# A conditioned two-part block on one core: conditioning bias from compact rows, a seeded fourth output tile, and a re-ordered weight load

## The chip, the cores and the metric

The kernel runs on one core of one Trainium2 chip. The core has five engines with instruction queues of their own: TensorE (PE: matrix products; PEld is its weight load), VectorE (DVE), ScalarE (ACT), GpSimd (POOL) and SyncE (SP, which here only issues transfers). Each runs its instructions in order and waits on counters that the others raise. Sixteen DMA engines move data between memory (DRAM) and on-chip memory; products land in PSUM banks. The metric is the device time of one execution in microseconds.

## The reference

```python
m = mask[:, :, None]                                   # x: 32 x 128 x 512, mask: 32 x 128
emb = silu(t) @ ada_w + ada_b                          # t: 32 x 512, ada_w: 512 x 1536
shift, scale, gate_msa = split(emb, 3, axis=1)
norm = layernorm(x) * (1 + scale[:, None]) + shift[:, None]
norm = where(m, norm, 0)
fwd = gelu(norm @ ssm_w1 + ssm_b1) @ ssm_w2 + ssm_b2
bwd = ...                                              # the same with the bwd_ weights
x = x + gate_msa[:, None] * where(m, fwd + bwd, 0)
ff_ada = silu(t) @ ffada_w + ffada_b
shift_mlp, scale_mlp, gate_mlp = split(ff_ada, 3, axis=1)
ff_norm = layernorm(x) * (1 + scale_mlp[:, None]) + shift_mlp[:, None]
h = gelu_tanh(ff_norm @ ff_w1 + ff_b1)                 # 512 x 1024
return x + gate_mlp[:, None] * (h @ ff_w2 + ff_b2)     # 1024 x 512
```

All is float32. The first part changes only the tokens whose mask is set, at most the last 32 of a sequence of 128. The second part is done for all 4096 tokens.

## The kernel before

**First part.** The masked tokens are gathered into 512 slots, four tiles of 128 (an indirect transfer by POOL, L281). Tiles 0 and 1 (group s0) go first, tiles 2 and 3 (s1) follow. Each group is normalised, transposed (`transposed_slots`, L192), sent through the hidden layer (`ph_s`, L656 and L207) and through the output product `project` (L217: eight matmuls of 128x512 into a bank `po_s`, half of them on `ssm_w2`, half on `bwd_w2`). A bank can be *seeded*: ACT copies the bias `b2` into it beforehand (L236), and the product adds onto it. In the kernel before, tiles 0 to 2 are seeded; tile 3 is not, its bank comes from another pool, and `finish_late` (L1364) adds `b2` on DVE. The finished rows go to DRAM: `x1_wide` (tiles 0 and 1, L368, read back at L792 for the first eight sequences) and `x1_rows` (all four, L369 and L1371, read back by POOL's eight gathers of `take_first_half`, L864).

**Conditioning.** `modulation_matmuls` (L299) makes shift, scale and gate for all 32 batches: for each of four column blocks j, 32 output partitions, sixteen matmuls of 32 columns for the four row blocks k of `ada_w`. `modulation_rows` (L311) adds the bias on DVE, from a tile in which each bias row stands on 32 partitions (`load_conditioning_bias`, L129: one broadcast transfer of 64 KB for each of three rows, twice). `pm_ss` is shift and scale of the first part, `pm_g` its gate, `pm_f` all three of the second part, `mod1` and `mod2` the results. `keep_clock` (L596) issues matmuls whose result nobody reads.

**Second part.** Both products are done by blocks: seven products P1 to P7 in place of eight, at two levels in the first product. There, seven *streams* (order 1, 2, 5, 6, 3, 7, 4) of seven products each run over the tokens of a pair of sides; there are four pairs. Streams 5, 6, 7 and 4 use sums of weight blocks, which DVE makes (L715), SP stores to `t_rows` (L719, L720) and `load_weights` (L1037, its transfer is L1042, tile `tw`) reads back. `token_sums` (L1015, `sx` and `xn_sy`) makes the token side on DVE. After P5 of a stream, `with_p5` (L1144) adds two 128x512 blocks on POOL at L1147; `after` (L1171) adds another on POOL at L1176. The result of a POOL sum goes through DVE (L1121 after P6; `seed`, L1136, at L1140 before P2) into the bank that the next product adds onto.

**What sets the order.** From L428 on the order of every engine is the order of the program text (a schedule by hand). Each transfer on the queues of SP and ACT takes one of eight completion counters in turn, and a transfer waits until the one that had its counter before has landed.

Around the switch from the first part to the second, SP issues in this order: load of `fw2` (L136), six stores of weight sums (L719, L720), two stores of `x1_rows` (L369), `b2_row`, `fb2`, two loads of x (L396), two stores of `x1_rows` (L1371), `tw` for stream 5 (L1042), two loads of x, `tw` for stream 6.

Of the kernel before, what the change touches and what calls it, by code (L numbers as in the profile page):

```python
# [9 lines left out]
F32 = mybir.dt.float32  # L10
# [4 lines left out]
ALU = mybir.AluOpType  # L15
# [7 lines left out]
def kernel(  # L23
# [49 lines left out]
    nc = tc.nc  # L73
    B, S, D = x.shape
    P = 128
# [3 lines left out]
    KC = D // P  # L79
# [46 lines left out]
        for k in blocks:  # L126
            nc.sync.dma_start(t[:, k, :width], w[ts(k, P), :width])

    def load_conditioning_bias(t, vec, kinds, queue):  # L129

        rows = vec.rearrange("(m j c) -> m j c", m=3, c=P)
        for m in kinds:
            queue.dma_start(t[:, m], rows[m].unsqueeze(1).to_broadcast([KC, B, P]))

    def load_blocks(t, w):
        nc.sync.dma_start(t, w.rearrange("(k p) f -> p k f", p=P))  # L136

    def load_behind_gathers(t, w):
        nc.gpsimd.memset(t[0:1, 0, 0:1], 0.0)
        load_blocks(t, w)  # L140

    modb_a = adap.tile([P, 3, P], F32, tag="modb", name="modb_a", bufs=1)
    n_bias = 2 * KC + HC
    bias_rows = ssm.tile([n_bias, P], F32, name="bias_rows")
    col = {"ssm1": 0, "bwd1": KC, "ff1": 2 * KC}
# [2 lines left out]
    w2 = ssm.tile([P, HC, D], F32, name="w2")  # L148
    ada_a = adap.tile([P, KC, 3 * D], F32, tag="ada", name="ada_a")
    load_ada(ada_a, ada_w, range(2), 2 * D)  # L150
    load_conditioning_bias(modb_a, ada_b, range(2), nc.sync)
    load_ada(ada_a, ada_w, range(2, KC), 2 * D)


# [14 lines left out]
    def own_statistics(t, n, name):  # L169

        for i in range(n):
            st = stp.tile([P, 6], F32, tag="st", name=f"st_{name}_{i}")
            row = t[:, i]
            nc.vector.bn_stats(st, row[:, :D])
            nc.vector.bn_aggr(row[:, D : D + 2], st)
        var = t[:, :, D + 1]
        nc.vector.tensor_scalar(var, var, EPS, None, ALU.add)
        nc.gpsimd.tensor_tensor(var, var, half[:, :n], ALU.pow)
# [38 lines left out]
    def project(i, h, w, name, between=None, bank=(ps_o, "o"), seeded=None):  # L217

        pool, tag = bank
        po = seeded or pool.tile([P, 512], F32, tag=tag, name=f"po_{name}_{i}")  # L220
        for f in range(HC):
            if between and f in between:
                between[f]()
            nc.tensor.matmul(  # L224
                po,
                h[f][:, ts(i, P)],
                w[:, f, :],
                start=(f == 0 and seeded is None),
                stop=(f == HC - 1),
                skip_group_check=seeded is not None,  # L230
            )
# [61 lines left out]
    def gather_slots(token_i):  # L293
        both = xp.tile([P, 2, D], F32, tag="x", name=f"xc_{len(xc)}")
        for c in range(NC // 2):
            gather(both[:, c], token_i[:, c : c + 1])
            xc.append(both[:, c])

    def modulation_matmuls(pm, ada, lo, hi, blocks):  # L299
        kinds = ada.rearrange("p k (m d) -> p k m d", d=D)  # L300
        for k in blocks:
            for j in range(KC):
                nc.tensor.matmul(
                    pm[ts(j, B), : (hi - lo) * P],
                    sT[:, k, :],
                    kinds[:, k, lo:hi, ts(j, P)],
                    start=(k == 0),
                    stop=(k == KC - 1),
                )

    def modulation_rows(pm, mod, modb, lo, hi):  # L311
        view = pm[:, : (hi - lo) * P].rearrange("p (m c) -> p m c", c=P)
        nc.vector.tensor_tensor(mod[:, lo:hi], view, modb[:, lo:hi], ALU.add)

    def of_slots(picked, tiles, mod, kinds, banks, name):

# [45 lines left out]
    def finish_slots(at, po, gate):  # L362
        t = tp.tile([P, 1, D + 2], F32, tag="t", name=f"t_s_{at}")
        row = t[:, 0, :D]
        nc.vector.tensor_tensor(row, po, gate, ALU.mult)
        nc.vector.tensor_tensor(row, row, xc[at], ALU.add)
        own_statistics(t, 1, f"s_{at}_x1")
        nc.sync.dma_start(x1_wide[ts(at, P), :], t[:, 0])  # L368
        return lambda: nc.sync.dma_start(x1_rows[ts(at, P), :], row)  # L369
# [141 lines left out]
    for j in range(2):  # L511
# [4 lines left out]
            start=True,  # L516
# [31 lines left out]
    for key, vec in (("ssm1", ssm_b1), ("bwd1", bwd_b1), ("ff1", ff_b1)):  # L548
# [1 line left out]
        nc.scalar.dma_start(  # L550
            bias_rows[col[key] : col[key] + n, :], vec.rearrange("(c p) -> c p", p=P)
        )
    load_conditioning_bias(modb_a, ada_b, (2,), nc.scalar)

    every = adap.tile([B, 3, P], BF16, name="every")
    nc.vector.memset(every, 1.0)
    for j, batches in ((1, 2 * G), (2, G)):
        nc.gpsimd.affine_select(
            out=every[:, j],
            in_=every[:, j],  # L560
            compare_op=ALU.is_gt,
            fill=0.0,
            base=batches,
            pattern=[[0, P]],
            channel_multiplier=-1,
        )
# [29 lines left out]
    def keep_clock(n, k):  # L596
        for _ in range(n):
            for j in range(KC):
                nc.tensor.matmul(
                    pm_keep_clock[ts(j, B), : 2 * P],  # L600
                    sT[:, k, :],
                    ada_a[:, k, ts(j, 2 * P)],
                    start=True,
                    stop=True,
                )

    pm = ps_o.tile([P, 512], F32, tag="o", name="pm_ss")
    for k in range(KC):
        modulation_matmuls(pm, ada_a, 0, 2, (k,))
        if k < KC - 1:  # L610
            keep_clock(1, k)
    slots_of_late = slots_to_count(pick[:, NH:], NC // 2, "s1", (ps_h, "h"))
    nc.vector.tensor_scalar(modb_a[:, 1], modb_a[:, 1], 1.0, None, ALU.add)
    modulation_rows(pm, mod1, modb_a, 0, 2)

    strips = of_slots(pick, (0, 1), mod1, slice(0, 2), 3 * [(ps_o, "o")] + [(ps_h, "h")], "part_s0")
    keep_clock(1, 0)
    xT_s = ssm.tile([P, KC, NH], F32, tag="xT", name="xT_s0", bufs=2)
    xT_t = ssm.tile([P, KC, NH], F32, tag="xT", name="xT_s1", bufs=2)
    xn = group_of_tiles("s")  # L620
# [20 lines left out]
    load_raw(2)  # L641
    load_raw(3)
    ada_f = adap.tile([P, KC, 3 * D], F32, tag="ada", name="ada_f")
    modb_f = adap.tile([P, 3, P], F32, tag="modb", name="modb_f", bufs=1)
    load_conditioning_bias(modb_f, ffada_b, range(3), nc.gpsimd)
    load_ada(ada_f, ffada_w, range(KC), 3 * D)
    ph_s = {}

# [24 lines left out]
        hidden_of_tile(f, 0)  # L673
    transposed_slots(xn_s[1], xT_s[:, :, ts(1, P)], "s1")
    pm = ps_o.tile([P, 512], F32, tag="o", name="pm_g")
    modulation_matmuls(pm, ada_a, 2, 3, range(KC))
    modulation_rows(pm, mod1, modb_a, 2, 3)

# [38 lines left out]
    def store_weight_sums(*which, queue=nc.sync):  # L717
        for j in which:
            queue.dma_start(t_rows[j - 1, :, 4:], t_sum[j][1][:, :3])  # L719
            queue.dma_start(t_rows[j - 1, :, :4], t_sum[j][0])  # L720
# [59 lines left out]
    own_statistics(raw[2], 2, "x_2")  # L780
    b2_row = dram.tile([1, D], F32, name="b2_row")
    store_rows = [finish_slots(0, project(0, h1, w2, "s0", seeded=po_s[0]), gs[0])]
    own_statistics(raw[3], 2, "x_3")
    t = in_blocks(group_of_tiles("tw_3"))
    t_sum[3] = [t[:, :4], t[:, 4:]]
    weight_sums(3)
    store_weight_sums(3)
    nc.vector.tensor_scalar(modb_f[:, 1], modb_f[:, 1], 1.0, None, ALU.add)

    def take_first_rows(i):  # L790
        slots = P if i < G else NH
# [16 lines left out]
        transposed_slots(xn_late[c], xT_t[:, :, ts(c, P)], f"s{2 + c}")  # L808
    mod2 = const.tile([P, 3, P], F32, name="mod2")
    pm = ps_h.tile([P, 512], F32, tag="h", name="pm_f")  # L810
    modulation_matmuls(pm, ada_f, 0, 3, range(KC))

    def in_turned_blocks(t):
# [13 lines left out]
    def normalised_of_side_0(which):  # L827
        for i in which:
            t = normalised(raw[i // 2][:, i % 2], xn[:, :, i])
            nc.vector.transpose(t, t)  # L830

    normalised_of_side_0(range(1))
    modulation_rows(pm, mod2, modb_f, 0, 3)
    normalised_of_side_0(range(1, 2))
    weight_sums(1)
    normalised_of_side_0(range(2, G))
    early.close()
# [504 lines left out]
    def turn_rows(b):  # L1342
        return lambda: turned(xn, xT[0], (nc.sync, nc.scalar), (b,))

    def load_of_pair_1():
# [7 lines left out]
        3: [turn_rows(0), lambda: weight_sums(4)],  # L1353
        4: [turn_rows(1)],
        5: [turn_rows(2)],
        6: [turn_rows(3), lambda: load_behind_gathers(fw2, ff_w2), lambda: store_weight_sums(4, 1, 2)] + store_rows,
        7: [load_of_pair_1],
    }
    h1 = hidden(xT_t, NH, w1, 0, AF.Gelu, "s1", ssm, after=after)
# [1 line left out]
    for k in range(KC):  # L1361
        scaled(0, xT[0], k)

    def finish_late(at, po, bias=None):  # L1364
        t = tp.tile([P, D], F32, tag="t", name=f"t_s_{at}")
        if bias is not None:
            nc.vector.tensor_tensor(t, po, bias, ALU.add)
            po = t
        nc.vector.tensor_tensor(t, po, gs[at], ALU.mult)
        nc.vector.tensor_tensor(t, t, xc[at], ALU.add)  # L1370
        nc.sync.dma_start(x1_rows[ts(at, P), :], t)  # L1371

    finish_late(2, project(0, h1, w2, "s2", {2 * k: turn(k) for k in range(KC)}, seeded=po_s[2]))
    po = project(1, h1, w2, "s3", bank=(ps_h, "h"))
    of_x[0] = TokenBlocks(0, xT)
    for j in (1, 2):
        of_x[0].one(j)
    fw2_of.combine(0, 1)
    for j in (3, 4):
        of_x[0].one(j)  # L1380
    finish_late(3, po, b2)
    first_half.close()
    hp = straight.enter_context(tc.tile_pool(name="hp", bufs=1))
    gp = straight.enter_context(tc.tile_pool(name="gp", bufs=1))
    now = FirstProduct(0, of_x[0].cut(), of_w)
    now.load_weights(1)
    x_of[1][1] = load_side(1, 1)
    now.load_weights(2)
    for n in range(2):
        now.token_sums(1, n)  # L1390
    now.apart(1)
    now.do(1, "P1")
    now.seed(1)
# [1 line left out]
    now.do(1, "P5", "P2", "P6")  # L1395
    now.do(2, "P5")
    now.seed(2)
    now.do(1, "P3")
    now.with_p5(2, "12")
    now.do(1, "P7")  # L1400
# [267 lines left out]
```

## Time and profile before

| | us |
|---|---|
| median of three runs (lowest, highest) | 457.97 (457.69, 458.17) |
| the profiled execution, its own time | 457.94 |
| its span, first to last instruction | 456.2 |
| PE busy in the span | 445.3 (98%) |
| DVE, ACT, POOL busy | 332.8, 176.9, 161.2 |
| first matmul of stream 5 | starts at 97.33 |

1.74 us of the profiled execution lie outside its span. The page gives the share of busy time of each engine, the span in 40 slices, the transfers, the chain that ended last, and the costliest groups. Times below count from the start of the span. A row of the timeline reads: start, length, engine, line, operation, what it writes and reads, shapes, and in brackets how long the engine had been idle before and what ended that.

The granted clock of TensorE is 0.999 of full speed over the whole span; the page shows no slice below nine tenths.

### The profile page before, as it was taken

Reading aid. Unit: us, or ns where it says so; the run is one execution under the profiler, and the core shown is the slowest. Engines: PE = TensorE matmul, PEld = TensorE weight load, DVE = VectorE, ACT = ScalarE, POOL = GpSimd, SP = SyncE. Lnnn points to the kernel's source line nnn. Section 1 sums busy time; section 2 is a strip of 40 time slices with the busy share of each in tenths; the row PEclk is TensorE's granted clock in tenths of the full one; section 3 lists DMA queues with packets and bytes.
Section 4 is the critical chain, followed back from the end, with each engine's and each line's share of the span. In section 5 each row is a group of like instructions: output and inputs, shape, how many; then the busy total and the mean of one; then the engine's idle time right before and its main releaser. Section 6 shows DMA issues by size and latency. Waiting matters only on the chain.

```text
span 456.2 us, 6196 instructions
## 1 busy us (share of the span) xinstructions
PE 445.3 (98%) x2161; PEld 370.9 (81%) x2161; DVE 332.8 (73%) x570; ACT 176.9 (39%) x387; POOL 161.2 (35%) x155
## 2 busy tenths in 40 slices
PE   8999999979999999999999999999999999999995
PEld 4784485668888888888888888888888888888884
DVE  4797887978779749895796398867963995534645
ACT  3123126244543551545435515454355154552000
POOL 4230560079770000697700006977000027560000
PEclk9999999999999999999999999999999999999999
DMA  7999549982208725822187258221772442222022
GB/s 233 382 352 403 232 70 261 339 343 96 80 22 221 115 60 203 290 96 82 34 214 106 64 198 293 94 84 43 201 111 62 152 149 82 80 92 94 0 93 96
DMA packets 83201, 70.98 MB, mean 156 GB/s; under 512 B 63292, under 2 KB 64268, under 8 KB 82142
## 3 DMA queue, kind: packets, MB, share of 16 engines
q1 hardware_dynamic: 67994, 58.41, 41.0%
q0 software_dynamic: 4400, 10.74, 7.0%
q10 hardware_dynamic: 10772, 1.39, 2.2%
q8 instruction: 19, 0.31, 0.3%
q14 instruction: 16, 0.13, 0.1%
HBM read 56.84 MB, written 13.70 MB: 155 GB/s over the span
## 4 chain that ended last, share of the span: by engine, by line
PE 80%; DMA 13%; DVE 4%; SPq 1%; issue 1%; POOL 0%; ACT 0%; POOLq 0%; ACTq 0%; DVEq 0%
PE a_o L1283 23%; PE a_m L1096 20%; PE e_o L1283 18%; PE e_m L1096 15%; DMA fw<-in_L_cond_ff_w_dram 7%; DMA tw<-t_rows 2%; DMA w<-in_L_cond_ssm_w_dram 1%; PE ph_s L207 1%; DVE t L387 1%; DMA xT<-xn 1%; DMA x_wide<-t_s 1%; PE last L1283 1%; SPq L935 1%; DMA x<-x_wide,slot_i 1%; DVE fw L387 0%
## 5 line engine op out<-in xcount | busy, mean ns | idle before, releaser
L1147 POOL TENSOR_TENSOR ha<-p_m,ha 128x512 f32<-128x512 f32 x20 | 25.8, 1289 | 176.8 <-ACT ha L1154 167.4
L1283 PE MATMUL e_o<-fw,ha 128*128 128x256 f32 x256 | 57.9, 379 | 0.0
L918 ACT ACTIVATE xT<-xT,modT 128x128 f32<-128x128 f32 x112 | 44.0, 480 | 33.0 <-DMA xT<-xn 32.1
L1283 PE MATMUL a_o<-t,hb 128*128 128x256 f32 x240 | 54.1, 379 | 0.0
L1283 PEld LDWEIGHTS e_o<-fw,ha 128*128 128x128 f32 x256 | 48.7, 190 | 6.5
L1283 PEld LDWEIGHTS a_o<-t,hb 128*128 128x128 f32 x240 | 45.7, 190 | 6.1
L1058 ACT ACTIVATE hb<-hb,biasT 128x256 f32<-128x256 f32 x64 | 29.0, 500 | 27.9 <-POOL hb L1180 19.4
L1110 ACT COPY p_m<-e_m 128x512 f32<-128x512 f32 x27 | 15.8, 585 | 50.1 <-PE e_m L1096 50.1
L864 POOL DMA_INDIRECT x<-x_rows,slot_i x24 | 28.5, 1186 | 6.8 <-issue 4.9
L224 PE MATMUL po_s<-w,h_s 128*128 128x512 f32 x64 | 28.7, 596 | 0.9 <-DMA w<-in_L_cond_bwd_w_dram 0.9
L1147 POOL TENSOR_TENSOR hb<-p_m,hb 128x512 f32<-128x512 f32 x20 | 29.4, 1470 | 0.3
L1283 PE MATMUL a_o<-t,s 128*128 128x256 f32 x128 | 28.9, 380 | 0.0
L1283 PE MATMUL a_o<-fw,ha 128*128 128x256 f32 x128 | 28.9, 379 | 0.0
L1283 PE MATMUL e_o<-fw,s 128*128 128x256 f32 x128 | 28.9, 379 | 0.0
L1154 ACT COPY ha<-e_m 128x512 f32<-128x512 f32 x32 | 18.5, 579 | 25.2 <-PE e_m L1096 24.7
L1283 PEld LDWEIGHTS a_o<-t,s 128*128 128x128 f32 x128 | 24.4, 190 | 3.2
L1283 PEld LDWEIGHTS a_o<-fw,ha 128*128 128x128 f32 x128 | 24.4, 190 | 3.3
L1283 PEld LDWEIGHTS e_o<-fw,s 128*128 128x128 f32 x128 | 24.4, 190 | 3.2
L1121 DVE TENSOR_TENSOR e_m<-a_m,ha 128x512 f32<-128x512 f32 x20 | 13.9, 697 | 16.7 <-POOL ha L1147 6.6
L1058 ACT ACTIVATE ha<-e_m,biasT 128x256 f32<-128x256 f32 x48 | 20.0, 467 | 14.7 <-PE e_m L1096 12.5
L1096 PE MATMUL a_m<-xT,tw 128*128 128x256 f32 x96 | 24.7, 380 | 0.0
L1126 DVE TENSOR_TENSOR hb<-a_m,hb 128x512 f32<-128x512 f32 x20 | 13.7, 685 | 15.0 <-PE a_m L1096 15.0
(235 smaller groups left out, 904.5 us busy)
## 6 DMA issues: line engine op xcount, KB each, us to landing
tw<-t_rows SPq DMA_DIRECT2D x16, 896.0 KB, 5.5
x<-in_x_dram SPq DMA_DIRECT2D x16, 512.0 KB, 12.0
gate<-gate_rows POOLq DMA_DIRECT2D x8, 1024.0 KB, 5.2
out_dram<-x SPq DMA_DIRECT2D x15, 512.0 KB, 4.4
xT<-xn SPq DMA_DIRECT2D x92, 64.0 KB, 2.4
fw<-in_L_cond_ff_w_dram SPq DMA_DIRECT2D x2, 2048.0 KB
ada_f<-in_L_cond_ffada_w_dram SPq DMA_DIRECT2D x4, 768.0 KB, 13.9
ada_a<-in_L_cond_ada_w_dram SPq DMA_DIRECT2D x4, 512.0 KB, 5.3
```

The costliest lines, as they stand in the source:

```text
L207: nc.tensor.matmul(ph[:, :n], w[:, k, ts(f, P)], xT[:, k, :], start=(k == 0), stop=(k == KC - 1))
L224: nc.tensor.matmul(po, h[f][:, ts(i, P)], w[:, f, :], start=(f == 0 and seeded is None), stop=(f == HC - 1), skip_group_check=seeded is no ...
L864: nc.gpsimd.indirect_dma_start(out=xs[i // G][i % G // 2][:, i % 2], out_offset=None, in_=x1_rows, in_offset=bass.IndirectOffsetOnAxis(ap= ...
L918: nc.scalar.activation(out, src, AF.Identity, bias=shift, scale=scale)
L1058: nc.scalar.activation(dst[:, n], src[:, n], AF.Gelu_apprx_tanh, bias=biasT[:, f : f + 1])
L1096: nc.tensor.matmul(bank[:, ts(n, QT)], self.w_block(j, product)[:, ts(n, P)], self.x_block(j, product), start=(product in ("P1", "P5") and ...
L1110: nc.scalar.copy(p5, e)
L1121: nc.vector.tensor_tensor(e, a, p5, add)
L1126: nc.vector.tensor_tensor(dst, a, dst if prior else self.p5[j], add)
L1147: nc.gpsimd.tensor_tensor(self.place(RESULT[j], c), self.p5[j], other, ALU.add)
L1154: nc.scalar.copy(self.place(RESULT[j], c), src)
L1283: nc.tensor.matmul(part, src[:, k, ts(i, P)], w[product][:, k, :], start=(last and k == 0), stop=True, skip_group_check=True,)
```

## The change

1. The two bias vectors are loaded as compact rows: two transfers at the head of ACT's queue put row j of vector r on partition 32 j + r of one tile `modb`. DVE adds 1 to the four pairs of scale rows. Four matmuls of two rows each (a row of the identity picks the vector) write the bias into the bank first, and the sixteen matmuls add onto it. `modulation_rows` is then a copy. The six broadcast transfers and the two DVE additions of 128x128 are gone.
2. The three groups of `keep_clock` between the row blocks of `pm_ss` are gone, and the group after `part_s0` is doubled.
3. The copy to `mod2` stands ahead of the first normalisation of the second part on DVE.
4. Tile 3 is seeded like the others and its bank comes from the same pool. On DVE its finish stands ahead of the last two token sums of `TokenBlocks`.
5. The two late stores of `x1_rows` are kept in `store_rows` and issued behind `load_weights(1)`; the first two token sums of stream 5 stand behind `seed(2)`.

```diff
-    def load_conditioning_bias(t, vec, kinds, queue):
-
-        rows = vec.rearrange("(m j c) -> m j c", m=3, c=P)
-        for m in kinds:
-            queue.dma_start(t[:, m], rows[m].unsqueeze(1).to_broadcast([KC, B, P]))
...
-    modb_a = adap.tile([P, 3, P], F32, tag="modb", name="modb_a", bufs=1)
+    modb = adap.tile([P, 3, P], F32, name="modb")
+    AT_A, AT_F = range(2)
+    for at, vec in ((AT_A, ada_b), (AT_F, ffada_b)):
+        nc.scalar.dma_start(
+            modb.rearrange("(j r) m c -> j r m c", r=B)[:, at],
+            vec.rearrange("(m j c) -> j m c", m=3, c=P),
+        )
...
     load_ada(ada_a, ada_w, range(2), 2 * D)
-    load_conditioning_bias(modb_a, ada_b, range(2), nc.sync)
     load_ada(ada_a, ada_w, range(2, KC), 2 * D)
...
+    def modulation_bias(pm, at, lo, hi):
+        for j in range(KC):
+            pair = slice(j * B, j * B + 2)
+            nc.tensor.matmul(
+                pm[ts(j, B), : (hi - lo) * P],
+                ident[pair, j * B + at : j * B + at + 1].to_broadcast([2, B]),
+                modb[pair, lo:hi],
+                start=True,
+                stop=True,
+                skip_group_check=True,
+            )
+
     def modulation_matmuls(pm, ada, lo, hi, blocks):
...
-                    start=(k == 0),
-                    stop=(k == KC - 1),
+                    start=False,
+                    stop=True,
+                    skip_group_check=True,
                 )
-    def modulation_rows(pm, mod, modb, lo, hi):
+    def modulation_rows(pm, mod, lo, hi):
         view = pm[:, : (hi - lo) * P].rearrange("p (m c) -> p m c", c=P)
-        nc.vector.tensor_tensor(mod[:, lo:hi], view, modb[:, lo:hi], ALU.add)
+        nc.vector.tensor_copy(mod[:, lo:hi], view)
...
-    load_conditioning_bias(modb_a, ada_b, (2,), nc.scalar)
     every = adap.tile([B, 3, P], BF16, name="every")
     nc.vector.memset(every, 1.0)
+    for j in range(KC):
+        scale = modb[j * B : j * B + 2, 1]
+        nc.vector.tensor_scalar(scale, scale, 1.0, None, ALU.add)
...
-    for k in range(KC):
-        modulation_matmuls(pm, ada_a, 0, 2, (k,))
-        if k < KC - 1:
-            keep_clock(1, k)
+    modulation_bias(pm, AT_A, 0, 2)
+    modulation_matmuls(pm, ada_a, 0, 2, range(KC))
     slots_of_late = slots_to_count(pick[:, NH:], NC // 2, "s1", (ps_h, "h"))
-    nc.vector.tensor_scalar(modb_a[:, 1], modb_a[:, 1], 1.0, None, ALU.add)
-    modulation_rows(pm, mod1, modb_a, 0, 2)
+    modulation_rows(pm, mod1, 0, 2)
...
-    keep_clock(1, 0)
+    keep_clock(2, 0)
...
-    load_conditioning_bias(modb_f, ffada_b, range(3), nc.gpsimd)
...
+    modulation_bias(pm, AT_A, 2, 3)
     modulation_matmuls(pm, ada_a, 2, 3, range(KC))
...
     store_rows = [finish_slots(0, project(0, h1, w2, "s0", seeded=po_s[0]), gs[0])]
+    po_s.append(seeded_with_bias(3))
...
-    nc.vector.tensor_scalar(modb_f[:, 1], modb_f[:, 1], 1.0, None, ALU.add)
...
+    modulation_bias(pm, AT_F, 0, 3)
     modulation_matmuls(pm, ada_f, 0, 3, range(KC))
...
-    normalised_of_side_0(range(1))
-    modulation_rows(pm, mod2, modb_f, 0, 3)
-    normalised_of_side_0(range(1, 2))
+    modulation_rows(pm, mod2, 0, 3)
+    normalised_of_side_0(range(2))
...
-    def finish_late(at, po, bias=None):
+    def finish_late(at, po):
         t = tp.tile([P, D], F32, tag="t", name=f"t_s_{at}")
-        if bias is not None:
-            nc.vector.tensor_tensor(t, po, bias, ALU.add)
-            po = t
         nc.vector.tensor_tensor(t, po, gs[at], ALU.mult)
         nc.vector.tensor_tensor(t, t, xc[at], ALU.add)
-        nc.sync.dma_start(x1_rows[ts(at, P), :], t)
+        store_rows.append(lambda: nc.sync.dma_start(x1_rows[ts(at, P), :], t))
...
-    po = project(1, h1, w2, "s3", bank=(ps_h, "h"))
+    po = project(1, h1, w2, "s3", seeded=po_s[3])
...
     fw2_of.combine(0, 1)
+    finish_late(3, po)
     for j in (3, 4):
         of_x[0].one(j)
-    finish_late(3, po, b2)
...
     now.load_weights(1)
+    for g in store_rows[2:]:
+        g()
     x_of[1][1] = load_side(1, 1)
     now.load_weights(2)
-    for n in range(2):
-        now.token_sums(1, n)
     now.apart(1)
...
     now.seed(2)
+    for n in range(2):
+        now.token_sums(1, n)
     now.do(1, "P3")
```

More of the change, by code (lines that the diff above doesn't have):

```diff
@@ L643 @@
     ada_f = adap.tile([P, KC, 3 * D], F32, tag="ada", name="ada_f")
-    modb_f = adap.tile([P, 3, P], F32, tag="modb", name="modb_f", bufs=1)
-    load_conditioning_bias(modb_f, ffada_b, range(3), nc.gpsimd)
     load_ada(ada_f, ffada_w, range(KC), 3 * D)
@@ L675 @@
     pm = ps_o.tile([P, 512], F32, tag="o", name="pm_g")
+    modulation_bias(pm, AT_A, 2, 3)
     modulation_matmuls(pm, ada_a, 2, 3, range(KC))
-    modulation_rows(pm, mod1, modb_a, 2, 3)
+    modulation_rows(pm, mod1, 2, 3)
     whole = "p i (b g f) -> p b i g f"
@@ L1355 @@
         5: [turn_rows(2)],
-        6: [turn_rows(3), lambda: load_behind_gathers(fw2, ff_w2), lambda: store_weight_sums(4, 1, 2)] + store_rows,
+        6: [turn_rows(3), lambda: load_behind_gathers(fw2, ff_w2), lambda: store_weight_sums(4, 1, 2)] + store_rows[:2],
         7: [load_of_pair_1],
```

## The prediction

> **What bounds the kernel now.** I first asked for the busy time in two stretches, before and after stream 5 begins, then for what PE waited on before it. (Windows: stretch, its length, then each engine's busy time and instruction count, clock, DMA share, GB/s. Waits: total us, times, longest.)
>
> ```profile
> 0.00:97.30 97.30, 91.19 (x525) 60.10 (x526) 76.82 (x180) 29.12 (x63) 31.04 (x49) 1.00 0.86 292
> 97.30:451.50 354.20, 354.14 (x1636) 310.78 (x1636) 255.11 (x389) 147.77 (x324) 130.12 (x107) 1.00 0.41 119
> ```
>
> ```profile
> PE e_m L1096 <- DMA tw<-t_rows: 2.3, 1, 2.3
> ...
> PE po_s L224 <- DMA w<-in_L_cond_bwd_w_dram: 0.9, 1, 0.9
> PE e_m L1096 <- DVE e_m L1121: 0.6, 1, 0.6
> PE ptr_mod L845 <- DVE mod L313: 0.4, 1, 0.4
> ```
>
> From 97.3 on PE never stops: 354.14 of 354.20 us. So the change, which lies before that, can only move the moment from which PE runs through. It aims at all four waits. The next question is who else must be earlier if PE is; the timelines of SP, POOL, DVE and PE around stream 6 answer it.
>
> ```profile
> 87.39 1.55 SPq L1371 DMA_DIRECT2D x_rows<-t_s  x2
> 89.10 0.37 SPq L1042 DMA_DIRECT2D tw<-t_rows  x1
> ...
> 95.88 1.11 POOL L864 DMA_INDIRECT x<-x_rows,slot_i  x1 [0.66 <-DMA tw<-t_rows]
> ...
> 106.93 1.00 POOL L864 DMA_INDIRECT x<-x_rows,slot_i  x1 [0.30 <-issue]
> 107.95 1.28 POOL L1147 TENSOR_TENSOR ha<-p_m,ha 128x512 f32<-128x512 f32 x1
> 109.17 1.28 POOL L1147 TENSOR_TENSOR hb<-p_m,hb 128x512 f32<-128x512 f32 x1
> 110.40 1.27 POOL L1176 TENSOR_TENSOR ha<-ha 128x512 f32<-128x512 f32 x1
> ...
> 111.71 0.70 DVE L1140 TENSOR_TENSOR e_m<-a_m,ha 128x512 f32<-128x512 f32 x1 [0.57 <-POOL ha L1176]
> ...
> 112.94 1.03 PE L1096 MATMUL e_m<-xT,fw 128*128 128x256 f32 x4
> ```
>
> POOL is the engine to see here. Its eight gathers (L864) run one after the other from 95.88 to 107.93, and the sums of stream 6 start right behind them. DVE waits 0.57 us for the third of these sums, and its seed ends at 112.41 for a PE that takes it up at 112.94. **PE's slack there is 0.5 us** (0.48 after the 0.05 us that the row of 90.44 shows from DVE to PE). And the first gather waits for the stores of `x1_rows` (L1371): by the program's list of waits for both, not for `tw`, which the profile names but which lands only at 97.19 (89.10 plus its 8.1 to landing).
>
> **Bias transfers.** The six broadcasts go. What they cost is in the DMA queues, once for 4 to 8 us and once for 27 to 31 us (packets, MB, share of 16 engines):
>
> ```profile
> q1 hardware_dynamic: 540, 1.13, 85.0%
> ...
> q1 hardware_dynamic: 356, 0.86, 81.8%
> q0 software_dynamic: 236, 0.20, 23.0%
> ```
>
> In the second, q0 is almost all `modb_f` (it lands at 31.0, 22.79 + 8.2): 23.0% of 64 engine-us over 236 packets is 62 ns for one of 512 bytes. Its 384 packets cost 384 x 62 / 16 = 1.5 us of all engines. The Trainium skill speaks against so much: "DMA: Bandwidth & Descriptors", Specifications, gives 512 bytes as the least transfer for line rate; at the 393 GB/s that 20 to 24 us show, 196 KB would be 0.5 us. I take the row, rounded down to **1.4** (ends 0.5 and 1.8; 1.8 if all that 27 to 31 us moved below 393 GB/s is put down to them). The DMA engines are full from 11 to 49 us, so `fw1`, `bwd_w2` and `ada_f` land 1.4 us earlier. The broadcasts of `modb_a` stand between the `ada_a` loads; without them the last block is issued 1.3 us earlier and has 256 small packets less ahead of it (0.3 us by their 131 KB, 1.0 at 62 ns each), and lands near 9.3 instead of 11.2, but the engines then idle until `w1` is issued at 9.32, which POOL's first gather triggers: nothing for the DMA chain. POOL is also rid of 2.15 us of issue at 22.79, where it is idle anyway.
>
> **Added at the start.** Two more issues on ACT (0.26 to 0.50 us each, by the rows of the bias loads L550) delay the table load and Silu by 0.5 to 1.0 us; Silu ends at 3.40 and PE wants it at 4.27: 0 to 0.1, I take 0. Four additions on DVE, 0.2 us each like L613, fall into its pause from 5.55 to 6.58, unless `modb` lands late: they wait for both transfers, and the token count (L264), the gathers and `w1` stand behind them. Issued near 1.7 with 3.5 to landing like the first `ada_a` block: 5.2. Cost 0; if the cover is gone, up to 0.7.
>
> **pm_ss.** Twenty matmuls without the three groups between: five blocks of 0.85 us from 6.48 end near 10.75 instead of 12.12. `mod1` is ready 1.1 us earlier; xc_0 lands at 12.55 today against the tail of `ada_a` and should also come about 1 us earlier. Then `w1` (lands 15.96) decides, so PE's first half gains 0.8 us. Here the clock speaks: the same matmul took 635 ns up to 11 us and 378 behind.
>
> ```profile
> 6.40 1.08 PE L303 MATMUL pm_ss<-ada_a,sT 128*32 128x256 f32 x8
> ...
> 11.51 0.61 PE L303 MATMUL pm_ss<-ada_a,sT 128*32 128x256 f32 x8
> ```
>
> The skill's "TensorE: Matmul & The Clock Gate", Part 1, says that PE reaches its full clock only after some 3.4 us of sustained work; the taken-out `keep_clock` groups were such work. By the rule PE could stay at half clock one window longer, up to 3.4 us lost between 17 and 26; by the rows PE stays busy from 6.4 to 11.3 in the new order too (bias, 16, late slots), so I take 0 and keep the 3.4 as a rival.
>
> **pm_g, pm_f.** Four bias matmuls each: two passes of the 32 in 1.08 us and of 2.79 us, that is 0.1 to 0.3 and 0.35 to 0.65. I take 0.25 and 0.65; both on PE's path. `po_s0` is then ready for `bwd_w2` at 39.19 - 0.8 + 0.25 = 38.6, `bwd_w2` lands at 40.13 - 1.4 = 38.7: the 0.94 us wait goes, PE is 1.4 earlier. `pm_f` ends 1.4 - 0.65 = 0.75 earlier (53.5). The copy to `mod2` (0.52) ends at 54.05, the gather lands at 54.78 - 1.4 = 53.4: DVE starts to normalise 0.75 earlier, has 0.53 less between, and ends its transposes **1.2 earlier**; the 0.4 us wait of `ptr_mod` goes. Everything that SP issues from 62.24 on, `fw2` and the stores included, moves by D = 1.2 (0.3 to 1.6).
>
> **Tile 3.** DVE loses one 0.68 us addition, ACT gains a copy of 0.59 in its pause 38.5 to 51.2. The bank of stream 2's P1 is now tile 3's: freed by L1369 near 84, wanted then: 0 to 0.1. The moved token sums free L1121 1.3 us earlier: the 0.64 us wait goes. `sx` is done near 91, wanted near 94.
>
> **The load of stream 5.** `tw` is issued behind x instead of behind the row stores: near 86, not 89.10. In SP's queue 524 KB of stores no longer lie ahead (1.25 us at 420 GB/s): it lands at 97.19 - 1.25 - 1.2 = 94.7, and PE wants it near 93.4. `tw` for stream 6 lands at 102.3 (91.11 + 11.2) - 1.2 against 103.44 before: PE alone would gain 2.3 us, not more. But the **row stores** now stand behind 918 KB. All three together end when `tw` ended before: 97.19 - 1.2, and 0.1 for a write. Today the gather starts at 95.88 on them; then at about 96.15, **0.3 later**. POOL's gathers and sums keep their lengths, so the seed L1140 ends at 112.7, and PE takes it up at 112.75 instead of 112.94.
>
> **Sum.** Against the profiled 457.94 (the median, 457.97, is the same to 0.03): -0.48 of slack + 0.3 = -0.2, **457.7 us**. PE arrives some 2 us early at stream 6 and waits there for POOL. With D from 0.3 to 1.6 the first gather moves by +1.2 to -0.1, and eight gathers of 0.99 to 1.50 us may vary by 0.4: 456.9 to 459.0 for this case alone.
>
> **Rivals.** *POOL doesn't hold it* (chance 0.36): the row stores land no later than today (the queue's engines don't finish in the order of issue, or fewer KB of `tw` are ahead of them), or the gathers run shorter with less traffic beside them. For: landings 95.8 and 97.19 are only 1.3 us apart although 918 KB would take 2.2. Against: `x_rows` L369 took 14.0 us to land, so the order of the queue counts. Then `tw` of stream 6 decides: 457.94 - 2.0 = 455.9 in full, and 456.7 if only half.
>
> *The row stores land still later* (0.22, slower): one mechanism, their place behind `tw`. With no shift of SP's queue ahead of it (D = 0, by a late `modb`) they pay 1.4, and 2.2 if the whole of `tw` passes first: the first gather starts at 97.3 to 98.1, the end is 457.94 - 0.48 + 1.4 to 2.2 = 458.9 to 459.7. It decides from a first gather later than 97.3. With PE at half clock to 20 us (0.06 of it) D turns to about -2: 460.5.
>
> *No effect* (0.42), the forecast above.
>
> **Numbers.** A measurement here tells 0.2% (0.9 us) from no change. From the cases: faster 0.37, within 0.2% 0.41, slower 0.22. Cases of both signs hold the chance, so the range takes in the first rival in full and most of the second: 455.7 to 459.3.
>
> **What would show it.** In the changed profile: first gather (L864's successor) near 96.2 and stream 6's POOL sums near 108.2, directly behind the gathers; a PE wait of 1.5 to 2 us at P3 or P2 of streams 6 and 3, where none is now; the waits of 0.9, 0.6 and 0.4 gone, that on `tw` 1.3; `fw1` used near 36.0. It is wrong if POOL's sums start before 107.4, if PE shows no wait behind 105 us, or if the DMA rate at 27 to 31 us is still 268 GB/s.

## The result and the profile after

| | before | after |
|---|---|---|
| median (lowest, highest), seven runs each | 458.17 (457.66, 459.12) | 462.07 (460.08, 464.06) |
| ratio of after to before, 95% interval | | 1.0079 (1.0053 to 1.0105) |
| the profiled execution, its span | 457.94, 456.2 | 462.75, 461.0 |
| P1 of stream 1 starts on PE | 84.45 | 87.51 |
| first of the eight row gathers starts on POOL | 95.88 | 101.45 |
| POOL's sums of stream 6 start | 107.95 | 112.61 |

The changed kernel is 3.9 us slower. Two of its parts cost time, at two places some 80 us apart. (Lines of the changed kernel are some ten higher than before: the weight load is L1052, the row stores L1378, the gathers L874, POOL's sums L1157 and L1186. In single runs of later kernels the granted clock fell to 0.99, and in one to 0.56 (789 us, not in its ratio), which makes any kernel longer.)

**The start.** From the timeline of the changed kernel, rows of ACT, SP, DVE and POOL (start, length, engine, line, what is written from what; in brackets the idle time before it and what ended it):

```profile
1.26 1.90 SPq L127 DMA_DIRECT2D ada_a<-in_L_cond_ada_w_dram  x4
...
1.28 1.14 ACTq L139 DMA_DIRECT2D modb<-in_L_cond_ada_b_dram  x1
2.45 0.56 ACTq L139 DMA_DIRECT2D modb<-in_L_cond_ffada_b_dram  x1
...
8.24 0.97 DVE L570 TENSOR_SCALAR modb<-modb 2x128 f32<-2x128 f32 x4 [2.76 <-DMA modb<-in_L_cond_ffada_b_dram]
9.24 0.42 DVE L263 TENSOR_TENSOR before_s<-pl_s,slot_col 128x254 f32<-128x254 f32 x1
...
10.61 1.19 POOL L280 DMA_INDIRECT xc<-in_x_dram,token_i_s  x1 [4.52 <-DVE inside L248]
...
11.97 0.39 SPq L130 DMA_DIRECT2D w<-in_L_cond_ssm_w_dram  x1
```

The token count and the first token gather in the kernel before:

```profile
6.58 0.42 DVE L264 TENSOR_TENSOR before_s<-pl_s,slot_col 128x254 f32<-128x254 f32 x1 [1.04 <-PE pl_s L258]
...
7.95 1.19 POOL L281 DMA_INDIRECT xc<-in_x_dram,token_i_s  x1 [1.79 <-DVE inside L249]
```

In the changed kernel DVE stands still for 2.76 us until the second compact load has landed, 5.8 us after its issue began. The token count (L263) is behind it: 9.24 instead of 6.58. The first token gather follows, 10.61 instead of 7.95, and with it the load of `w1`, 11.97 instead of 9.32. What that means for the DMA engines is in the table of stretches of the same run (stretch, length, busy time and instructions of PE, PEld, DVE, ACT, POOL, granted clock, DMA share, GB/s):

```profile
8.00:10.00 2.00, 1.49 (x8) 0.70 (x8) 1.60 (x6) 0.00 (x0) 0.00 (x0) 1.00 0.23 91
10.00:12.00 2.00, 2.00 (x22) 0.83 (x24) 1.77 (x7) 0.00 (x0) 1.32 (x2) 1.00 0.00 0
27.00:31.00 4.00, 4.00 (x35) 3.34 (x34) 2.73 (x8) 1.18 (x3) 0.71 (x1) 1.00 1.05 390
```

Before, these three stretches moved 273, 244 and 268 GB/s. The last line is the saving that the removal of the broadcasts brought: by estimate (390 - 268) x 4 / 400 = 1.2 us of all engines. The first two are what it cost: the engines now do nothing for most of 8 to 12 us, and from 16 us on are full to 45.

PE meets the loss twice. First it waits for `modb` itself, and `ph_s` begins at 18.65 instead of 16.88. Then the loads behind `w1` are late too: DVE stands still for 1.93 us until a load of x lands at 28.13, and what it makes after that holds PE up once more:

```profile
37.76 1.90 PE L338 MATMUL gate_s<-mod,pick 32*128 32x128 f32 x32 [1.39 <-DVE x L356]
```

That makes up the 3.06 us by which P1 of stream 1 is later: 1.77 at `ph_s`, 1.39 here and 1.13 for the added bias matmuls of `pm_g` and `pm_f`, less the waits of 0.94 and 0.4 that are gone, together 2.9.

**The switch.** What PE waited for, in the changed kernel (total us, times, longest):

```profile
PE e_m L1106 <- DMA tw<-t_rows: 1.6, 1, 1.6
PE gate_s L338 <- DVE x L356: 1.4, 1, 1.4
PE pm_ss L301 <- DVE modb L570: 1.4, 1, 1.4
...
PE e_m L1106 <- DVE e_m L1131: 1.2, 1, 1.2
```

and the timeline of SP, POOL, DVE and PE there:

```profile
88.11 0.94 SPq L408 DMA_DIRECT2D x<-in_x_dram  x2
91.34 0.34 SPq L1052 DMA_DIRECT2D tw<-t_rows  x1
91.72 1.44 SPq L1378 DMA_DIRECT2D x_rows<-t_s  x2
...
101.45 1.59 POOL L874 DMA_INDIRECT x<-x_rows,slot_i  x1 [3.00 <-DMA x<-in_x_dram]
...
112.61 1.27 POOL L1157 TENSOR_TENSOR ha<-p_m,ha 128x512 f32<-128x512 f32 x1
...
113.91 0.70 DVE L1131 TENSOR_TENSOR e_m<-a_m,ha 128x512 f32<-128x512 f32 x1 [2.16 <-POOL ha L1157]
...
114.67 1.13 PE L1106 MATMUL e_m<-xn_sy,tw 128*128 128x256 f32 x4 [1.20 <-DVE e_m L1131]
```

POOL has been idle for 3 us when its first gather may start. The name in the bracket is that of a load of x; the gather has to wait for the row stores L1378, of which the second is issued at 92.6 and takes 8.1 us, to 100.7, and 0.8 us later the gather starts. From there the chain is the one that the prediction described: eight gathers back to back, the sums, DVE, PE. POOL's sums are 4.66 us later than before, PE had 0.48 us of slack, and the span grew by 4.8.

### The profile page after: what moved, and what is told of

Its sections match the earlier page's. It is cut to its first block, busy times and chain, and to the rows that moved or that the text cites. A ratio compares the mean times of both kernels' runs of the same rounds, so it can differ in the third digit from the quotient of the medians.

```text
span 461.0 us, 6202 instructions
## 1 busy us (share of the span) xinstructions
PE 447.3 (97%) x2169; PEld 370.5 (80%) x2169; DVE 332.9 (72%) x571; ACT 177.9 (39%) x388; POOL 158.8 (34%) x152
## 4 chain that ended last, share of the span: by engine, by line
PE 69%; DMA 11%; DVE 7%; POOL 4%; SPq 4%; ACT 3%; issue 2%; ACTq 0%; POOLq 0%; DVEq 0%
PE a_o L1293 17%; PE a_m L1106 17%; PE e_o L1293 13%; PE e_m L1106 13%; SPq L945 3%; PE ph_s L206 3%; PE po_s L223 3%; DMA x<-in_x_dram 3%; DMA t_rows<-tw_b 2%; DMA tw<-t_rows 2%; DMA b_row<-b 1%; ACT xT L928 1%; DMA modb<-in_L_cond_ffada_b_dram 1%; DMA xT<-xn 1%; POOL x L874 1%
## 5 line engine op out<-in xcount | busy, mean ns | idle before, releaser
L1157 POOL TENSOR_TENSOR ha<-p_m,ha 128x512 f32<-128x512 f32 x20 | 26.3, 1313 | 177.5 <-ACT ha L1164 167.9
L874 POOL DMA_INDIRECT x<-x_rows,slot_i x24 | 27.6, 1150 | 9.1 <-issue 5.1
L1157 POOL TENSOR_TENSOR hb<-p_m,hb 128x512 f32<-128x512 f32 x20 | 29.4, 1470 | 0.3
L1131 DVE TENSOR_TENSOR e_m<-a_m,ha 128x512 f32<-128x512 f32 x20 | 13.9, 697 | 19.7 <-POOL ha L1157 8.7
L1106 PE MATMUL e_m<-s,fw 128*128 128x256 f32 x92 | 23.8, 381 | 0.1
```

The lines of the kernel that those rows point to most:

```text
L874: nc.gpsimd.indirect_dma_start(out=xs[i // G][i % G // 2][:, i % 2], out_offset=None, in_=x1_rows, in_offset=bass.IndirectOffsetOnAxis(ap= ...
L1106: nc.tensor.matmul(bank[:, ts(n, QT)], self.w_block(j, product)[:, ts(n, P)], self.x_block(j, product), start=(product in ("P1", "P5") and ...
L1131: nc.vector.tensor_tensor(e, a, p5, add)
L1157: nc.gpsimd.tensor_tensor(self.place(RESULT[j], c), self.p5[j], other, ALU.add)
```

## The experiments

Theory L: the late `modb` holds the token count and with it the chain of loads. Theory R: the row stores, now behind `tw`, land later. Theory C: PE's own start is slower, by a cold clock and added matmuls.

**Each half alone.** The kernel before with parts 1 to 3 of the change, and with parts 4 and 5:

> The kernel before with the compact bias rows alone (loads on ACT, four additions ahead of the token count, bias matmuls); row stores, stream 5's weights and the fourth tile as before. Theory L (the late modb holds up the token count, and with it w1 and the whole chain of loads): token count near 9.2 instead of 6.6, the first gather of rows near 98.9 instead of 95.9, total about 460.9. Theory R (the row stores behind tw alone cost the time): nothing of the loss is here, 457.5 to 458.5. Theory C (PE's own start: no clock-keeping matmuls, 635 ns ones, added bias matmuls): about 459.5 to 461 too, but with the token count's delay not deciding: w1 lands as before.

> The kernel before with the other two parts alone: fourth tile seeded, row stores of tiles 2 and 3 behind stream 5's weights, token sums moved; broadcasts as before. Theory L: first gather of rows at 96 to 97.3, total 457.2 to 459.0. Theory R (the place behind tw costs 2 us or more by itself): first gather at 98 or later, PE waits over 1 us in streams 6 and 3, total 459.5 to 460.5. Theory C: as theory L, 457.2 to 459.0.

The compact rows alone: 459.51 us, ratio 1.0034 (1.0021 to 1.0047). The tail alone: 460.18, ratio 1.0055 (1.0040 to 1.0071). Together 1.0089, against 1.0079 measured for the whole: **two costs that add up**, about 1.6 and 2.2 us. Neither theory alone holds; each half showed its own mark. With the compact rows alone PE waits 0.8 us for `modb` and 1.3 at `gate_s`, runs pm_g's and pm_f's bias matmuls on top, and begins P1 of stream 1 at 86.80 (84.45 before), while the first gather, at 97.68, starts 0.25 us after POOL's own sums. With the tail alone P1 begins at 84.98, and the gather is late by itself: at 97.15 in the profiled run, which is the fastest of the six (458.73), so there it is still inside theory L's forecast; the median is theory R's. The timeline and one wait of SP in the run of the tail alone, and the landing of its row stores:

```profile
88.40 0.34 SPq L1043 DMA_DIRECT2D tw<-t_rows  x1
88.78 1.17 SPq L1369 DMA_DIRECT2D x_rows<-t_s  x2
```

```profile
SPq L1043 <- DMA b_row<-b: 1.5, 1, 1.5
```

```profile
DMA to landing us min/median/max: 6.8/6.8/6.8
```

`tw` is issued only 0.7 us earlier than before (89.10), not 3 us: SP waits 1.5 us (2.2 in the change) for the landing of `b_row`, a store of one 2 KB row. By the program's list of waits `tw` waited for that before too, but then the row stores were issued meanwhile; now they stand behind it.

**The start put right, step by step.** First the additions behind the token count; then, instead, the compact rows on SP ahead of `ada_a`:

```diff
-    for j in range(KC):
-        scale = modb[j * B : j * B + 2, 1]
-        nc.vector.tensor_scalar(scale, scale, 1.0, None, ALU.add)
...
     token_i = tokens_of(pick[:, :NH], slot_col[:, : NC // 2], NC // 2, "s0", ssm)
+    for j in range(KC):
+        scale = modb[j * B : j * B + 2, 1]
+        nc.vector.tensor_scalar(scale, scale, 1.0, None, ALU.add)
```

> The changed kernel with the four additions on DVE put behind the token count; the loads stay on ACT. Theory L: the token count waits only for the later Silu (0.75 us), first token gather near 8.7 instead of 10.6, w1 issued near 10.1 instead of 12.0, total about 1.9 less than the changed kernel: 460.1. Theories R and C: no more than 0.3 less, 461.8 to 462.1, since pm_ss still waits for modb.

```diff
-        nc.scalar.dma_start(
+        nc.sync.dma_start(
             modb.rearrange("(j r) m c -> j r m c", r=B)[:, at],
```

> The changed kernel with the two compact loads on SP, ahead of the ada_a loads, instead of on ACT. Theory L: modb lands near 5, Silu is back at 3.4, the token count at 6.6, first token gather near 8, pm_ss begins near 6.5; total 2.7 to 3.5 less than the changed kernel: 458.6 to 459.4, what is left being the row stores. Theory R: first gather of rows still over 99, total over 460.5. Theory C: pm_ss still 635 ns a matmul, ends near 11, and no more than 1 us less: 461.

Additions behind the count: the first token gather came at 8.60 as expected, the total did not (462.42). The compact rows on SP: DVE adds at 5.43 with no wait and the count is at 6.54, exactly as forecast for a `modb` in time, but the total is 461.47 (ratio 1.0075, 1.0038 to 1.0112), not 459. Theory L alone **missed** both times; the first gather at 99.32 is what theory R had forecast for the early rows. PE's rows in the run with early rows on SP say why:

```profile
10.03 1.08 PE L314 MATMUL pm_ss<-ada_a,sT 128*32 128x256 f32 x8 [0.62 <-DMA ada_a<-in_L_cond_ada_w_dram]
11.36 1.08 PE L314 MATMUL pm_ss<-ada_a,sT 128*32 128x256 f32 x8 [0.24 <-DMA ada_a<-in_L_cond_ada_w_dram]
...
13.38 1.91 PE L338 MATMUL part_s<-mod,pick 32*128 32x256 f32 x13
```

Now PE waits for `ada_a` between the row blocks, where the taken-out `keep_clock` groups had kept it at work, and the sixteen strip matmuls (`part_s`) behind it stretch over 2.3 us (12.99 to 15.29) instead of 1.15: one takes 629 ns in the median, in the change 374. `ph_s` begins at 19.16 (16.88 before). In the run with late additions PE still waits for `modb`, and `ph_s` is at 19.42. So theory C is a part of it; the groups went back in, once with the early rows and once alone:

```diff
-    modulation_matmuls(pm, ada_a, 0, 2, range(KC))
+    for k in range(KC):
+        modulation_matmuls(pm, ada_a, 0, 2, (k,))
+        if k < KC - 1:
+            keep_clock(1, k)
```

> The changed kernel with the compact rows loaded on SP ahead of ada_a, and with the three groups of clock-keeping matmuls back between the blocks of pm_ss. Theory C (with PE's short stops between the blocks its matmuls fall back to 635 ns; that ate what the early modb gave): the 16 strip matmuls take 1.15 us instead of the 1.9 without the groups, ph_s begins near 17 instead of 19.2, stream 5's or 1's P1 0.5 to 1.5 earlier than without them. If not C: ph_s still begins near 19. The total stays under theory R in either case: 460.0 to 461.5, first gather over 98.

> The changed kernel with the three groups of clock-keeping matmuls back, modb still loaded on ACT. In the changed kernel PE runs the blocks of pm_ss one behind the other, since all ada_a blocks have landed while it waits for modb, and its strip matmuls take 1.15 us; so theory C expects no gain here: total 461.5 to 463.5, the groups only add 2.5 us of PE work ahead of mod1. If the missing groups cost by themselves: 460.5 or less.

With early rows and groups: 459.65, ratio 1.0030 (1.0017 to 1.0043), `ph_s` at 16.89, P1 of stream 1 at 84.12, the first gather at 97.43; total and gather are lower than forecast (460.0 and 98 at least). The strips again:

```profile
12.67 1.15 PE L338 MATMUL part_s<-mod,pick 32*128 32x256 f32 x16
```

With the groups alone: 462.43, ratio 1.0081 (1.0055 to 1.0106), no gain, as theory C expected while `modb` is late. **The early `modb` alone and the groups alone gain nothing that can be measured; both together take away the loss of the start.** What is left, 0.3%, is the tail.

Slow strips are not bound to an early `modb`, though. Of the six profiled kernels with compact rows and without the groups, the sixteen strips took 1.15 us in three (the change, the compact rows alone, and "stores first" below) and 1.9 to 2.3 us in the other three. One of these, "`b_row` early" below, has the very start of the change, and no stop of PE behind the wait for `modb`:

```profile
14.47 1.68 PE L338 MATMUL part_s<-mod,pick 32*128 32x256 f32 x13
```

In all five profiled kernels with the groups back the strips took 1.15. In one of these five, with the stores on ACT's queue, the blocks of `pm_ss` themselves stayed slow to 13 us, and `ph_s` came at 18.27 in spite of early rows and groups.

**The tail.** The row stores ahead of `tw` again, in the changed kernel; then the order of the change, but the wait for `b_row` taken away by an early store:

```diff
+    for g in store_rows[2:]:
+        g()
     now.load_weights(1)
-    for g in store_rows[2:]:
-        g()
```

> The changed kernel with the row stores of tiles 2 and 3 issued ahead of stream 5's weights, as before; everything else as changed. Theory R (the load of tw, issued ahead, waits 2.2 us for the landing of the small store b_row and holds the row stores behind it; its bytes then lie ahead of theirs): stores issued by 90.8 instead of 92.6, landing near 6 us instead of 8, first gather of rows near 98.5 (then held by POOL's own sums to 98.45) instead of 101.45; tw issued no later than 91.5; total 458.8 to 459.7, and the runs lie within 2 us instead of 4. Theory L (the late modb alone): no more than 0.5 less than the changed kernel.

```diff
     b2_row = dram.tile([1, D], F32, name="b2_row")
+    nc.sync.dma_start(b2_row, b2[0:1, :])
...
-        nc.sync.dma_start(b2_row, b2[0:1, :])
         broadcast_rows(fb2, ff_b2, nc.sync)
```

> The changed kernel with the small store b_row issued where its buffer is declared, long ahead, so that tw no longer waits for its landing; the order tw, then row stores, stays. Theory R with the wait as its main part: tw issued near 89.3 instead of 91.3, row stores near 90.7 (they still wait for the stores of t_rows), first gather 99.5 to 100.5, total 460.4 to 461.2. Theory R with the bytes of tw ahead as its main part: stores land 8 us or more after issue, first gather over 100.5, total 461.5 to 462.5.

Stores first: 459.81, ratio 1.0042 (1.0027 to 1.0058), 0.1 above the forecast and in line with the compact rows alone. The runs spread by 3.1 us, more than the 2 expected: in the profiled one `modb` landed later still (first token gather at 11.72). `b_row` early: 462.16, ratio 1.0101 (1.0064 to 1.0137), no gain. `tw` went out at 87.72 and the stores at 88.18 and 89.6 (the second held 0.9 us by a store of `t_rows`), yet they took 8.0 us. So the wait for `b_row` is real in the trace, but by the median not what decides. The profiled run, one of the fastest of the six (460.52), had its first gather at 98.42, 3.0 earlier than the change and earlier than either forecast, so the share of this wait stays open. What decides is the order, and the fourth tile has no part that can be measured:

> The kernel before with the fourth tile seeded and its row finished earlier, and the token sums moved, but row stores ahead of stream 5's weights and broadcasts as before. If only the order of the row stores costs in that part of the change: total 457.2 to 458.4, that is no loss and little gain, first gather 95.2 to 96. If the seeding or the moved sums cost too: 459 or more, as with the order changed (460.2).

This is the tail alone with the stores ahead of `tw`: 458.57 us, ratio 1.0002 (0.9986 to 1.0019). The first gather, at 96.78, is later than forecast (95.2 to 96): POOL's second sum waits 1.23 us for a DVE addition that stands behind the moved token sums. The total shows no cost of it. In the profile:

```profile
87.62 2.01 SPq L1369 DMA_DIRECT2D x_rows<-t_s  x2
89.80 0.37 SPq L1043 DMA_DIRECT2D tw<-t_rows  x1
```

```profile
DMA to landing us min/median/max: 5.8/5.8/5.8
```

The profiled runs side by side (but for the one with the stores on ACT's queue; the two with all put right come below); the last column is the first gather less P1 of stream 1, which takes the start of the kernel out of it:

| kernel | row stores | P1 of stream 1 | first gather | difference |
|---|---|---|---|---|
| before | ahead of `tw` | 84.45 | 95.88 | 11.4 |
| compact rows alone | ahead | 86.80 | 97.68 | 10.9 |
| seed and order of DVE alone | ahead | 85.06 | 96.78 | 11.7 |
| change, stores first | ahead | 88.14 | 99.85 | 11.7 |
| all put right | ahead | 83.94 | 95.05 | 11.1 |
| all put right, `b_row` early | ahead | 84.13 | 95.84 | 11.7 |
| tail alone | behind | 84.98 | 97.15 | 12.2 |
| change, additions late | behind | 86.25 | 98.83 | 12.6 |
| change, groups back | behind | 86.35 | 99.10 | 12.8 |
| change, rows early, groups back | behind | 84.12 | 97.43 | 13.3 |
| change, rows early | behind | 85.99 | 99.32 | 13.3 |
| change | behind | 87.51 | 101.45 | 13.9 |
| change, `b_row` early | behind | 86.48 | 98.42 | 11.9 |

Ahead, the difference is 10.9 to 11.7, and there POOL's own sums end only 0.16 to 0.66 us before the gather may start. Behind, it is 11.9 to 13.9, and POOL is idle for 0.4 to 3.0 us: the means are 11.4 and 12.9, so the place behind `tw` costs some 1.4 us (12.86 - 11.43), and it varies more. Counted from P1, the stores land 9.5 to 10.1 us later ahead of `tw` (three runs where the profile gives it) and 11.1 to 13.2 behind it (six runs); in all six the gather follows the landing by 0.8 to 0.9 us. Counted from their issue the two overlap: 5.8, 5.9 and 8.1 (all put right, `b_row` early) ahead, 6.8 to 8.1 behind. The 918 KB of `tw` are 2.2 us at the 412 GB/s that 40 to 45 us show.

A profiled run is one draw: that of "groups back" took 459.62, the median of its kernel is 462.43. The medians of three pairs that differ in this order alone carry the conclusion. Ahead and behind, the ratios are 1.0002 and 1.0055 (fourth tile and order of DVE), 1.0042 and 1.0079 (the change), 0.9999 and 1.0030 (rows early, groups back): 1.4 to 2.4 us each. In the first pair the intervals are apart; in the other two they meet or overlap a little.

**Another queue, and all of it put right.** The same order with the stores on ACT's queue (early rows, groups back); and early rows, groups back and stores first on SP:

```diff
-        store_rows.append(lambda: nc.sync.dma_start(x1_rows[ts(at, P), :], t))
+        store_rows.append(lambda: nc.scalar.dma_start(x1_rows[ts(at, P), :], t))
```

> Early modb on SP and clock-keeping groups as in the run with all three put right, stream 5's weights first in SP's queue as in the change, but the row stores of tiles 2 and 3 issued from ACT's queue, so that they don't stand behind tw in SP's. If their place in SP's queue is the cost: they land near 6 us after issue, first gather of rows at 95 to 96.3, total 457 to 458.5. If the cost is that tw's bytes move at the same time, whatever the queue: landing 7.5 us or more, first gather 97 or later, total 459 or more. ACT's own next copy waits up to 1.5 us for the last of DVE's additions, 0.5 us of the total at most.

> The changed kernel with all three put right: compact rows loaded on SP ahead of ada_a, clock-keeping groups back, row stores ahead of stream 5's weights. If L, R and C together are the cause: first gather of rows at 95.3 to 96.2, total 456.8 to 458.2, so no slower than the kernel before, and at best 1 us faster, since POOL's gathers and sums still set the end. If something else costs the time (added matmuls on PE's path, the copy on ACT): 459 or more.

> The run with all three put right, and the small store b_row issued where its buffer is declared as well, so that neither tw nor ACT's first copy for stream 5 can wait for its landing. In the run with all three put right PE waited 1.8 us for tw at stream 5 and for nothing later. If tw's issue is what is left: tw issued near 87.3 instead of 88.0, PE's wait for it 1.0 to 1.5, total 456.7 to 457.4, 0.2% faster than the kernel before. If POOL's gathers and sums take over at once: 457.3 to 458.0, no difference that can be measured.

On ACT's queue the stores landed in 6.2 us and the first gather came at 96.20, as forecast for their place in SP's queue as the cost. But this run can't decide it: the second load of x took the completion counter of one of the stores, so that `tw`, meant to go first, went out at 93.53, when the stores had landed (86.7 + 6.2 = 92.9), and PE waited 3.6 us for it. ACT's queue also stood at the stores from 79.87 to 87.1, waiting for DVE. The median of 461.16 (ratio 1.0050, 1.0029 to 1.0070) holds these waits, and a granted clock below 0.997 in 13 of 22 runs besides; the nine others have a median of 458.68. **Whether it is the place in the queue or the bytes of `tw` moving at the same time stays open**; shown is the cost of the order.

With all three put right: 457.74, ratio 0.9999 (0.9982 to 1.0017). What PE waited for:

```profile
PE e_m L1109 <- DMA tw<-t_rows: 1.8, 1, 1.8
...
PE e_m L1109 <- DVE e_m L1134: 0.2, 1, 0.2
```

P1 of stream 1 is at 83.94, the first gather at 95.05, a little earlier than forecast, and from there on PE waits only for `tw` to speak of. The loss is gone; of a gain, 0.5 us at P1 is seen, and no difference in the total that can be measured. With `b_row` early on top, `tw` went out at 87.42 and PE waited 1.3, inside what was expected; the total of 458.22 is above both forecasts, but so is the kernel before in the same set (458.40): ratio 0.9995 (0.9976 to 1.0014). No version was measurably faster than the kernel before.

## Why the prediction was wrong

It forecast no effect, and the change made the kernel slower, beyond its range. Two terms were put at about nothing that cost some 2 us each: the landing of `modb` and the place of the row stores.

- **The step that failed first is "Added at the start".** It took `modb` to land at 5.2, "with 3.5 to landing like the first `ada_a` block", and a cost of 0, up to 0.7 "if the cover is gone". The two issues took 1.70 us instead of 0.5 to 1.0, and the second transfer landed 5.8 us after its issue began: the additions ended at 9.2, and the token count came 2.66 us late. The 0.7 counted only the additions, not the wait ahead of them. So D, by which SP's queue should have been 1.2 us earlier at the switch, was negative: the loads of x went out 1.7 us later (88.11 for 86.39), and P1 of stream 1 3.06 us later. The compact rows alone cost 1.6 us. With `modb` early (rows on SP) the step's picture was right to the row: additions at 5.43, count at 6.54.
- **"pm_ss" fell with it.** Blocks forecast to end near 10.75 ended at 13.9, at 634 ns a matmul throughout, and `mod1` was begun 1.8 us later instead of 1.1 earlier (the step's own figures, 12.12 and 10.75, give 1.4). The step kept PE busy through "bias, 16, late slots"; that holds only if neither `modb` nor a block is waited for. The rival of a slow PE, put at a chance of 0.06, named something real: strips of 590 to 629 ns in three of six profiled kernels. In the profiled run of the change they were fast.
- **"The load of stream 5" failed in two terms.** `tw` "issued near 86" went out at 88.40 with the tail alone and 91.34 in the change, in part by a wait on `b_row` (1.5 and 2.2 us) that the step had left out. And the gather behind the row stores, put at 0.3 later, is 1.4 us later on average and 2.5 in the profiled run (13.9 - 11.4), counted from P1. The step let all three transfers end together when `tw` ended before; with the tail alone the cost is 2.2 us.
- **The rival "the row stores land still later"** (0.22) named the second cost and even its worst case, "by a late `modb`". It was too small because it took the late `modb` only as a lost shift of SP's queue (D = 0). With the measured terms its sum comes out: 1.4 of its own, 1.7 by which SP's queue was late and 2.2 for `b_row` are 5.3 us (an estimate, since the terms may overlap), and the first gather was 5.6 us later.
- **Right:** that PE runs through from stream 5 on and that POOL's gathers and sums set its start with 0.48 us of slack (4.66 us later on POOL, 4.8 in the span; a wait of 1.2 at P3 of stream 6); the DMA time of the broadcasts (1.4 forecast, 1.2 by the rates between 27 and 31 us); the end of the waits for `bwd_w2`, `ptr_mod` and, at the switch, L1121, though the new wait at `gate_s` took back what the first two gave; no cost of seeding the fourth tile that could be measured. That the wait for `tw` fits (1.3 forecast, 1.6) is luck: `tw` landed, and PE wanted it, both over 4 us later than forecast. The bias matmuls were a little dear: pm_g 0.35 instead of 0.25, pm_f 0.78 instead of 0.65 on PE's path, and in `pm_ss` 1.74.

## What to carry to other kernels

A load that becomes an operand of an early instruction must be costed to its landing in the company it keeps, and every instruction behind the waiting one counts, down to the loads that these trigger. A transfer moved ahead of another in a queue takes its waits and its bytes along: ask who is behind it, and whether those are what the slowest engine waits for. A matmul that nobody reads may be what keeps the next ones fast, and one fast profiled run without it is no proof that it can go.

## What was not expected of the hardware

- The first compact load, of twelve rows of 512 bytes, took 1.14 us to issue on ACT and 0.72 on SP (the second 0.56 and 0.55), against 0.43 for the mask's load on ACT. Issued on ACT beside 2 MB of `ada_a` on SP, it landed with them (5.8 us for the second load, `ada_a` at a median of 6.5), and at different times from run to run: the first token gather, which waits for it, was at 10.06, 10.23, 10.24, 10.61 and 11.72 in five kernels with the same start up to there. Two rules of the Trainium skill bear on it ("DMA: Bandwidth & Descriptors", Queues, rings and completion order): that a DMA engine takes turns between queues, which would have let it pass early, and that the completion of a transfer lands only after every earlier write of that engine, across its queues, which would hold it. The late landing fits the second, but no run here separates the two from a plain shortage of rate.
- The length of PE's matmuls doesn't follow the granted clock of the table. In the run with early rows the granted clock reads 1.00 from 8 to 16 us, and yet the same strips took twice as long. The skill ("TensorE: Matmul & The Clock Gate", Part 1) has PE reach full speed after about 3.4 us of sustained work, with a window that runs freely. Here it took longer: with the stores on ACT's queue PE shows no stop from 5.20 us on, and its matmuls still took 634 ns up to 12.6; with `b_row` early it shows none from 8.14 on, and the strips from 14.08 still took 629 in the median. So the stops of 0.62 and 0.24 us in the run with early rows are not needed for slow strips, and what sets the moment of full speed is not shown here.
